# A graph layer on one core: row loads of SP taken out, 100 chunks of columns each on ScalarE and VectorE

## The chip, the cores and the metric

The kernel runs on one core of a Trainium2 chip. The time is the device time of one execution in microseconds (us); of several executions the median is given. The engines are named as the profile names them: PE (TensorE matmul, with its weight loads as PEld), DVE (VectorE), ACT (ScalarE), POOL (GpSimd) and SP (SyncE, which issues transfers). Each works through its own list of instructions in order.

## What is computed

One layer of a graph network over 12,500 nodes of 128 features and 200,000 edges that are sorted by their target `dst`:

```
h = maximum(layernorm(x), 0)
msgs = h[src]
agg = segment_sum(msgs, dst) / maximum(degree(dst), 1)
h = relu(agg @ Wg + h @ Ws + bg)          # 128 -> 128
h = tanh(h @ W1 + b1)                     # 128 -> 512
h = tanh(h @ W2 + b2)                     # 512 -> 512
out = x + h @ W3 + b3                     # 512 -> 128
```

All of it is in fp32. The inputs fix the edges, but the kernel may not rely on their values; it reads `src` and `dst` from memory.

## The kernel before

**Chunks.** The edges are cut into 1563 chunks of 128 (`NCH`). For each chunk the 128 rows `h[src]` have to be in SBUF, one edge to a partition. PE then multiplies them by a one-hot tile of 128 x 24 (`oh`, made by DVE for eight chunks at a time) and so adds them to the sums of the nodes of the current block. A block is 512 nodes, about 64 chunks, with smaller ones at the end (`blocks`). Sums of chunks that reach over two blocks are kept apart (`edge`).

**The start.** DVE and ACT normalise all rows in pieces and write them to a table in DRAM, `htab`. POOL meanwhile gathers the raw rows of ten groups of eight chunks (`raw_rows`, line 178), which are normalised later on DVE. After that the rows of `htab` are read back by blocks and turned on PE, and ACT copies them to `tab` (`own_turned`, line 700), a table in SBUF with the nodes along the free axis: one column of `tab` is one node's row.

**Four ways to the rows of a chunk.** They are what the change is about.

- *A gather* (line 385): POOL issues one indirect DMA a chunk, which fetches 128 rows of `htab` by the indices in `scol`. Tiles `rows`, `AHEAD` of them, and the gathers are written `AHEAD` chunks ahead of their use. 1323 chunks go this way.
- *Row loads* (`row_loads`, line 414): SP reads 32 offsets into registers and issues one transfer of 512 bytes for each row. 14 chunks. Tiles `srows`.
- *Column copies* (`column_copies`, line 435): ACT reads 16 offsets into registers and copies one column of `tab` for each edge, a 128 x 1 copy, into a tile `cols1`; `turn` (line 455) has PE transpose it and ACT copy the result to `turned`. 50 chunks.
- *Column pairs* (`column_pairs`, line 445): DVE reads 16 offsets and writes two columns with each of eight instructions into `cols2`; the second column of each pair is a sum of both, which `turn` undoes with a second matmul (`minus`). 96 chunks.

Every fourth chunk between `FROM` and `UNTIL` that isn't raw is a slot for one of the last three ways; `SHARES` says how many each gets, and they are spread evenly (lines 125 to 134).

**The order.** It is written out by hand in one loop over the chunks (line 882). `behind` counts the gathered chunks that PE has passed in this order. `load_times` (line 833) gives each group of copies a place in it: ACT's copies for a chunk stand between the chunk before of the same engine and the chunk itself, 18 gathers earlier (`MARGIN`), DVE's pairs 26 earlier (`MARGIN + GRP`). A block is turned nine gathers ahead of its use (line 849). The layers of a block begin `LEAD` chunks after its last chunk (line 926) and go on by one step in every two chunks (line 946). From chunk 1312 (`QUICK`) on, the steps are placed by a small sum of due times (line 918), since no more blocks follow to fill the time.

Of the kernel before, what the change touches and what calls it, by code (L numbers as in the profile page):

```python
# [22 lines left out]
F32 = mybir.dt.float32  # L23
# [8 lines left out]
P = 128  # L32
# [8 lines left out]
AHEAD = 24  # L41
LATE = 28
LEAD = 16
# [4 lines left out]
SHARES = 14, 50, 96  # L48
FROM, UNTIL = 104, 1540
SBUFS = 4  # L50
MARGIN = 18
TOGETHER = 4
LOADS = 32, 16, 16
# [24 lines left out]
def windowed(ctx, tc, x, src, dst, Wg, Ws, bg, W1, b1, W2, b2, W3, b3, out, flag):  # L78
# [46 lines left out]
    lanes = ([], [], [])  # L125
# [22 lines left out]
    rows_one = ctx.enter_context(tc.tile_pool(name="rows_one", bufs=SBUFS))  # L148
# [54 lines left out]
    ROWB = 4 * D  # L203
    places = [const.tile([NROW, CPR // EVERY, P], I32, name=f"place{i}") for i in range(2)]
# [37 lines left out]
    with tc.tile_pool(name="ln", bufs=2) as ln:  # L242

        def indices(name, a, pad, keep):
            r = sp.tile([NROW, ROW], I32, name="idx_raw")

            nc.vector.memset(r, pad)
            even = FULL // 16 * 16
            for s0, s1 in ((0, even), (even, FULL)):
                if s1 > s0:  # L250
                    nc.scalar.dma_start(r[s0:s1, :], a[s0 * ROW : s1 * ROW].rearrange("(p e) -> p e", e=ROW))
            nc.scalar.dma_start(r[FULL : FULL + 1, :REST], a[FULL * ROW : E].rearrange("(p e) -> p e", p=1))
            if name == "src":
                some = r.rearrange("r (q p) -> r q p", p=P)[:, AT::EVERY]
                nc.vector.tensor_scalar(places[0], some, float(ROWB), None, op0=ALU.mult)
                nc.vector.tensor_scalar(
                    places[1].rearrange("r q (i t) -> r q t i", t=2), some.rearrange("r q (t i) -> r q t i", t=2),
                    4.0, float(TAB_AT), op0=ALU.mult, op1=ALU.add,
                )
            else:  # L260
                r8 = sp.tile([NROW, ROW], U8, name="r8")
                nc.scalar.copy(r8, r.bitcast(U8).rearrange("r (e b) -> r e b", b=4)[:, :, 0])
                end = ahead_of + NROW * ROW
                nc.scalar.dma_start(bytes_at[ahead_of:end].rearrange("(r e) -> r e", e=ROW), r8)
                past = sp.tile([1, max(ahead_of, past_end)], U8, name="past")
                nc.vector.memset(past, PAST)
                nc.scalar.dma_start(bytes_at[:ahead_of].rearrange("(o e) -> o e", o=1), past[:, :ahead_of])
                nc.scalar.dma_start(bytes_at[end:].rearrange("(o e) -> o e", o=1), past[:, :past_end])
            rf = sp.tile([NROW, ROW], F32, name="idx_f")
            nc.vector.tensor_copy(rf, r)  # L270
            if name == "dst":
                by_chunk = rf.rearrange("r (q p) -> r q p", p=P)
                nc.vector.tensor_copy(firsts, by_chunk[:, :, 0])
                base = sp.tile([NROW, CPR], F32, name="base")
                nc.vector.tensor_tensor(base, firsts, lo, op=ALU.max)
                nc.vector.tensor_tensor(base, base, hi, op=ALU.min)
                nc.vector.tensor_copy(bases, base)
                nc.vector.tensor_tensor(  # L278
                    by_chunk, by_chunk, base[:, :, None].to_broadcast([NROW, CPR, P]), op=ALU.subtract
                )  # L280
            for q0 in range(0, CPR, 4):
                p = ps_m.tile([P, 4, P], F32, name="pm")
                for q in range(4):
                    nc.tensor.transpose(p[:, q, :NROW], rf[:, (q0 + q) * P : (q0 + q + 1) * P], ident[:NROW, :NROW])  # L284
                keep(q0, p[:, :, :NROW].rearrange("p q r -> p r q"))
# [73 lines left out]
    hbytes = htab.rearrange("n d -> (n d)").bitcast(U8)  # L359
# [34 lines left out]
    def offsets(lane, c, p0):  # L394
        step, first_at = (4, TAB_AT) if lane else (ROWB, 0)
        r, q = divmod(c, CPR)
        kind = (mybir.EngineType.SP, mybir.EngineType.Activation, mybir.EngineType.DVE)[lane]
        loads, vs = nc.values_load_multi_w_load_instructions(
            places[min(lane, 1)][r : r + 1, q // EVERY, p0 : p0 + LOADS[lane]], engines=[kind], min_val=first_at,
            max_val=first_at + (N - 1) * step,  # L400
            skip_runtime_bounds_check_because="src holds rows of x, as the indirect DMAs take it to",
        )
        for ld in loads:
            if lane == 2 and last:
# [5 lines left out]
        if lane:  # L410
            vs = [v.with_bounds(min_val=first_at, max_val=first_at + (N - 1) * step, guaranteed_mod_val=0, out_of_modulus=4) for v in vs]
# [15 lines left out]
    def two(lane, c, p0):  # L427
# [3 lines left out]
        for p in range(p0, p0 + LOADS[lane], 2):  # L431
            a, b = (tab[:, bass.ds((at_v[q] - TAB_AT) // 4, 1)] for q in (p, p + 1))
            yield p, by_pair[:, p // 2], a, b

    def column_copies():
        for c in lanes[1]:
            columns[c] = ed.tile([P, P], F32, name="cols1", bufs=3)
            for p0 in range(0, P, LOADS[1]):
                for p, to, *ab in two(1, c, p0):
# [5 lines left out]
    def column_pairs():  # L445
        for c in lanes[2]:
            columns[c] = ed.tile([P, P], F32, name="cols2", bufs=4)
            for p0 in range(0, P, LOADS[2]):
                for p, to, a, b in two(2, c, p0):
# [5 lines left out]
    def turn(c):  # L455

        pt, both = ps_m.tile([P, 4, P], F32, name="pm"), columns.pop(c)
        if c in lanes[1]:
# [374 lines left out]
    def load_times(lane):  # L833
# [12 lines left out]
    loading = [  # L846
        (loads, list(load_times(i))) for i, loads in enumerate((row_loads(0), column_copies(), column_pairs()))
    ]
    turns = sorted((max(1, sum(o < c for o in order) - MARGIN // 2), c) for c in sum(lanes[1:], []))
# [32 lines left out]
    for c in range(NCH):  # L882
# [14 lines left out]
        if c % (GRP // 2) == 0 and g + 2 < ngrp:  # L897
            copies, times = loading[2]
            while times and times[0] <= behind:
                times.pop(0)  # L900
                next(copies, 0)
# [6 lines left out]
        if not raw(c) and c not in apart:  # L908
            behind += 1
            for rows_of_lane, times in loading[:2]:  # L910
                while times and times[0] <= behind:
                    times.pop(0)
                    next(rows_of_lane, 0)
# [414 lines left out]
```

## Time and profile before

| | us |
|---|---|
| median of 3 runs | 1784.79 |
| lowest, highest run | 1784.59, 1784.84 |
| the profiled execution | 1782.46 |
| its span, first to last instruction | 1780.6 |
| POOL busy | 1334.6 |
| PE busy | 1424.5 |
| DVE busy | 1214.6 |
| ACT busy | 898.5 |

All figures of the engines below come from the one profiled execution. Busy times are the time in which at least one instruction of the engine ran. Matmuls overlap, and their ends are modelled, so that PE's busy time overstates how near it is to its peak. Register loads and the issue of transfers do not count as busy; a gap that they leave is put down to "issue". In a row of the timeline stand the start, the duration, the engine, the line, the operation, the tiles and the count, and in brackets the idle time ahead of it with what ended it. A row of the waits reads: who waited for what, us in total, times, the longest. A row of a stretch has the busy time of each engine with its instructions, and at its end the granted PE clock, the DMA share and GB/s; where one line was asked for, only its engine stands there.

### The profile page before, as it was taken

To read this page: it belongs to the slowest core of one execution; us is meant where nothing else is said; L and a number is where in the kernel's file an instruction comes from. 1 tells how busy PE (TensorE), PEld (TensorE's weight loads), DVE (VectorE), ACT (ScalarE), POOL (GpSimd) and SP (SyncE) were. 2 spreads that over 40 slices of the span, in tenths; PEclk is the share of its full clock that TensorE was granted. 3 is DMA by queue.
4 is the path that set the end of the run, shared out by engine and by line. 5 is a ranking of instruction groups with operands and counts; after the bars stand their busy time and mean duration, and the time that the engine had idled before them with its cause. 6 is when DMAs were issued, how large, how long until landed. Compare 5 with 4: busy or idle time off the path is not lost.

```text
span 1780.6 us, 35578 instructions
## 1 busy us (share of the span) xinstructions
PE 1424.5 (80%) x5696; PEld 942.3 (53%) x5696; DVE 1214.6 (68%) x6958; ACT 898.5 (50%) x6963; POOL 1334.6 (75%) x1411
## 2 busy tenths in 40 slices
PE   0047577878888898888988898888899899889798
PEld 0036455555555555455655655545556555555577
DVE  7965586786678676876768768777578675676520
ACT  1212254646546455554645545665546655656443
POOL 7777777777777777777777777777777777777774
PEclk9999999868877887986877877889778787889699
DMA  8945222222222222222222222222222222222221
GB/s 205 248 131 140 61 59 65 62 65 74 60 73 72 69 64 72 66 69 70 74 61 71 73 61 71 75 58 74 70 62 72 72 73 63 66 70 66 65 59 47
DMA packets 132964, 139.20 MB, mean 78 GB/s; under 512 B 31655, under 2 KB 109347, under 8 KB 132536
## 3 DMA queue, kind: packets, MB, share of 16 engines
q0 software_dynamic: 44896, 92.04, 20.5%
q1 hardware_dynamic: 84558, 41.29, 8.6%
q10 hardware_dynamic: 3276, 3.51, 0.7%
q14 instruction: 181, 1.48, 0.3%
q8 instruction: 53, 0.87, 0.2%
HBM read 123.71 MB, written 13.03 MB: 77 GB/s over the span
## 4 chain that ended last, share of the span: by engine, by line
PE 50%; DMA 28%; issue 14%; DVE 3%; POOL 3%; ACT 1%; SPq 0%; DVEq 0%; POOLq 0%; ACTq 0%
PE pm L377 35%; DMA rows<-htab,scol 25%; PE agg L377 11%; PE edge L377 4%; POOL rows L387 3%; DMA xt<-in_x_dram 2%; PE pm L380 1%; DVE cols L450 1%; DVE h L240 1%; DVE agg L226 1%; DVE agg L233 0%; DMA xb<-htab 0%; ACT h L472 0%; ACT cols L441 0%; DMA htab<-h 0%
## 5 line engine op out<-in xcount | busy, mean ns | idle before, releaser
L387 POOL DMA_INDIRECT rows<-htab,scol x1323 | 1253.8, 948 | 403.3 <-issue 225.6
L450 DVE SCALAR_TENSOR_TENSOR cols<-first_only,tab 128x2 f32<-128x2 f32 x6144 | 886.3, 218 | 222.9 <-issue 213.4
L377 PE MATMUL pm<-h,w 128*128 128x512 f32 (+4 forms) x1344 | 770.0, 673 | 2.8 <-ACT h L472 2.6
L441 ACT COPY cols<-tab 128x1 f32 x6400 | 652.2, 188 | 74.5 <-issue 67.0
L377 PEld LDWEIGHTS agg<-oh,rows 128*128 128x128 f32 x1914 | 382.7, 244 | 435.3 <-DMA rows<-htab,scol 256.8
L377 PE MATMUL agg<-oh,rows 128*128 128x24 f32 x1914 | 391.0, 303 | 176.8 <-DMA rows<-htab,scol 170.4
L377 PEld LDWEIGHTS pm<-h,w 128*128 128x128 f32 x1344 | 234.5, 220 | 15.2 <-issue 10.2
L377 PEld LDWEIGHTS edge<-oh,rows 128*128 128x128 f32 x732 | 138.0, 228 | 170.1 <-DMA rows<-htab,scol 100.2
L377 PE MATMUL edge<-oh,rows 128*128 128x24 f32 x732 | 146.3, 291 | 74.4 <-DMA rows<-htab,scol 69.8
L472 ACT ACTIVATE h<-pm,b2c 128x512 f32<-128x512 f32 (+4 forms) x112 | 70.8, 632 | 255.8 <-PE pm L377 254.8
L494 DVE TENSOR_TENSOR oh<-shared,dloc 128x192 f32<-128x192 f32 x186 | 65.0, 351 | 187.5 <-PE agg L377 109.1
L475 ACT COPY turned<-pm 128x128 f32<-128x128 f32 x146 | 38.1, 261 | 124.5 <-PE pm L377 101.7
L178 POOL DMA_INDIRECT raw<-in_x_dram,rsrc x80 | 80.0, 1000 | 25.8 <-issue 23.5
L472 ACT ACTIVATE h<-pm,b1c 128x512 f32<-128x512 f32 (+4 forms) x112 | 69.4, 631 | 43.9 <-PE pm L377 43.2
L534 DVE TENSOR_SCALAR_CACHE_REDUCE nearby<-nearby,parity 128x656 uint8<-128x656 uint8 x98 | 87.0, 887 | 0.0
L284 PE MATMUL pm<-ident,idx_f 98*128 98x98 f32 x32 | 5.7, 373 | 82.6 <-DVE idx_f L278 54.0
L472 ACT ACTIVATE h<-pm,b3c 128x512 f32<-128x512 f32 (+4 forms) x28 | 17.7, 633 | 94.1 <-PE pm L377 94.1
L377 PEld LDWEIGHTS agg<-oh,turned 128*128 128x128 f32 x194 | 43.7, 249 | 34.5 <-issue 33.0
L377 PE MATMUL pm<-ident,cols 128*128 128x128 f32 x192 | 51.6, 357 | 0.0
L377 PE MATMUL pm<-minus,cols 128*64 128x128 f32 x192 | 49.3, 345 | 0.0
L475 ACT COPY tab<-pm 128x512 f32<-128x512 f32 (+1 forms) x25 | 14.4, 577 | 68.8 <-PE pm L380 68.8
L284 PEld LDWEIGHTS pm<-ident,idx_f 98*128 98x128 f32 x32 | 5.2, 227 | 82.8 <-issue 54.2
(122 smaller groups left out, 904.9 us busy)
## 6 DMA issues: line engine op xcount, KB each, us to landing
srows<-htab SPq DMA_DIRECT2D x1792, 0.5 KB
rows<-htab,scol POOLq DMA_INDIRECT x1323
nearby<-bytes_at SPq DMA_DIRECT2D x98, 82.0 KB
xb<-htab SPq DMA_DIRECT2D x24, 256.0 KB
xb<-in_x_dram SPq DMA_DIRECT2D x23, 256.0 KB
out_dram<-o SPq DMA_DIRECT2D x23, 256.0 KB
xt<-in_x_dram SPq DMA_DIRECT2D x8, 640.0 KB
htab<-h SPq DMA_DIRECT2D x8, 640.0 KB
```

Source lines behind the costliest of these rows:

```text
L178: nc.gpsimd.indirect_dma_start(out=t[:, j, :], out_offset=None, in_=x, in_offset=bass.IndirectOffsetOnAxis(ap=rsrc[:, g, j : j + 1], axis=0),)
L226: nc.vector.tensor_reduce(stats[:, 0], xt, AX.X, ALU.add)
L240: nc.vector.scalar_tensor_tensor(h, xt, 0.0, spread(stats[:, 1], k), op0=ALU.max, op1=ALU.mult)
L377: tc.keep_in_program_order(nc.tensor.matmul(*a, **k))
L380: tc.keep_in_program_order(nc.tensor.transpose(*a, **k))
L387: nc.gpsimd.indirect_dma_start(out=r, out_offset=None, in_=htab, in_offset=bass.IndirectOffsetOnAxis(ap=scol[:, c : c + 1], axis=0),)
L441: tc.keep_in_program_order(nc.scalar.copy(to[:, t : t + 1], of))
L450: last[:] = [tc.keep_in_program_order(nc.vector.scalar_tensor_tensor(to, first_only, a, b.to_broadcast([P, 2]), op0=ALU.mult, op1=ALU.add))]
L472: tc.keep_in_program_order(nc.scalar.activation(*a, **k))
L475: tc.keep_in_program_order(nc.scalar.copy(*a))
L494: newest[:] = [nc.vector.tensor_tensor(oh[:, :k, :w], lane[:, None, :w].to_broadcast([P, k, w]), dloc[:, g * GRP : g * GRP + k][:, :, None ...
L534: done = nc.vector.tensor_scalar(w, w, parity[:, t % 2 : t % 2 + 1], None, op0=ALU.is_equal, op1=ALU.add, accum_out=found[:, t : t + 1])
```

## The change

Five settings change: `AHEAD` 24 to 30, `LEAD` 16 to 24, `FROM` 104 to 80, `SHARES` from 14, 50, 96 to 100, 100, and `LOADS` to 16 alone. SP's row loads and all that served them are taken out: the tiles `srows`, the second table of offsets with its DVE instruction, and their due times. The lanes are renumbered, ACT's columns from 1 to 0 and DVE's from 2 to 1. The code of the copies themselves stays. There are 345 slots now, the first in use chunk 87 on ACT and 91 on DVE; before, 339 and chunks 119 and 111. The last chunk of ACT is 1531 and of DVE 1535 in both.

```diff
-AHEAD = 24
+AHEAD = 30
 LATE = 28
-LEAD = 16
+LEAD = 24
...
-SHARES = 14, 50, 96
-FROM, UNTIL = 104, 1540
-SBUFS = 4
+SHARES = 100, 100
+FROM, UNTIL = 80, 1540
 MARGIN = 18
 TOGETHER = 4
-LOADS = 32, 16, 16
+LOADS = 16
...
-        kind = max(range(4), key=lambda k: owed[k])
+        kind = max(range(3), key=lambda k: owed[k])
         owed[kind] -= len(slots)
-        if kind < 3:
+        if kind < 2:
             lanes[kind].append(c)
...
-    rows_one = ctx.enter_context(tc.tile_pool(name="rows_one", bufs=SBUFS))
...
-                nc.vector.tensor_scalar(places[0], some, float(ROWB), None, op0=ALU.mult)
...
-    def row_loads(lane):
-        for c in lanes[lane]:
-            r = rows_one.tile([P, D], F32, name="srows")
-            rows_t[c] = r
-            rb = r.bitcast(U8)
-            for p0 in range(0, P, LOADS[0]):
-                for p, v in offsets(lane, c, p0):
-                    sp_dma(rb[p : p + 1, :], hbytes[bass.ds(v, ROWB)].rearrange("(o b) -> o b", o=1))
-                    if (p + 1) % TOGETHER == 0:
-                        yield
...
     def column_copies():
-        for c in lanes[1]:
+        for c in lanes[0]:
             columns[c] = ed.tile([P, P], F32, name="cols1", bufs=3)
...
     def column_pairs():
-        for c in lanes[2]:
+        for c in lanes[1]:
             columns[c] = ed.tile([P, P], F32, name="cols2", bufs=4)
...
-        use = [max(FROM - 46 + MARGIN, use[0] - step), *use] if lane else [use[0] - step * k for k in range(SBUFS - 1, 0, -1)] + use
-        if lane == 0:
-            use = [max(u, FROM // 2 + 7 * step // 8 * i) for i, u in enumerate(use)]
-        some = LOADS[2] if lane == 2 else TOGETHER
+        use = [max(FROM - 46 + MARGIN, use[0] - step), *use]
+        some = LOADS if lane else TOGETHER
         for i in range(len(lanes[lane])):
             for k in range(P // some):
-                yield max(1, use[i] + (use[i + 1] - use[i]) * k * some // P - (0, MARGIN, MARGIN + GRP)[lane])
+                yield max(1, use[i] + (use[i + 1] - use[i]) * k * some // P - (MARGIN + GRP if lane else MARGIN))
```

What it does to the lists of the engines, at three places. A row is a line of the program, an operation, the tile written and the one read, the size, and a count where it repeats; the line numbers of the changed kernel are smaller, by 18 near the copies.

POOL, from the last raw groups through all gathers of rows. Before:

```order
L178 DMA raw_156<-in_x_dram,rsrc 128x128 x8
L178 DMA raw_165<-in_x_dram,rsrc 128x128 x8
L178 DMA raw_174<-in_x_dram,rsrc 128x128 x8
L178 DMA raw_183<-in_x_dram,rsrc 128x128 x8
L387 DMA rows<-htab,scol 128x128 x1323
```

Now:

```order
L176 DMA raw_153<-in_x_dram,rsrc 128x128 x8
L176 DMA raw_162<-in_x_dram,rsrc 128x128 x8
L176 DMA raw_171<-in_x_dram,rsrc 128x128 x8
L176 DMA raw_180<-in_x_dram,rsrc 128x128 x8
L382 DMA rows<-htab,scol 128x128 x1283
```

The raw groups are as they were; 40 gathers are gone.

ACT, where the table is complete and the columns begin (`place` are the offsets that go to registers). Before:

```order
L475 COPY tab<-pm 128x512 x24
L475 COPY tab<-pm 128x256
L475 COPY sums<-edge 128x280
L475 COPY rd<-pm 128x512
L398 TENSOR_LOAD place_203
L441 COPY cols_1578<-tab 128x1 x16
```

Now:

```order
L457 COPY tab<-pm 128x512 x24
L457 COPY tab<-pm 128x256
L393 TENSOR_LOAD place
L423 COPY cols_1287<-tab 128x1 x16
L393 TENSOR_LOAD place
L423 COPY cols_1287<-tab 128x1 x16
```

The first copies stood behind the sums of the first block and its degrees, and now stand right behind the table.

ACT again, in the layers of the ninth block, from its first activation to the next one. Before:

```order
L472 ACTIVATE h_512_26993<-pm,bgc 128x512
L441 COPY cols_25892<-tab 128x1 x12
L398 TENSOR_LOAD place_203
L441 COPY cols_25892<-tab 128x1 x16
L398 TENSOR_LOAD place_203
L441 COPY cols_27264<-tab 128x1 x8
L472 ACTIVATE h_512_26997<-pm,b2c 128x512
```

Now:

```order
L454 ACTIVATE h_512_33401<-pm,bgc 128x512
L393 TENSOR_LOAD place
L423 COPY cols_33349<-tab 128x1 x16
L393 TENSOR_LOAD place
L423 COPY cols_33349<-tab 128x1 x8
L457 COPY turned<-pm 128x128
L423 COPY cols_33349<-tab 128x1 x8
L393 TENSOR_LOAD place
L423 COPY cols_33349<-tab 128x1 x16
```

Before, 36 copies and two register loads stand between the two activations. Now 88 copies, six loads and a turned block do, of which the piece shows the first 48 copies; the next activation, `h_512_33405<-pm,b2c`, comes after 40 more.

More of the change, by code (lines that the diff above doesn't have):

```diff
@@ L202, in windowed @@
     scol = const.tile([P, NCOL], I32, name="scol")
-    ROWB = 4 * D
-    places = [const.tile([NROW, CPR // EVERY, P], I32, name=f"place{i}") for i in range(2)]
+    place_of = const.tile([NROW, CPR // EVERY, P], I32, name="place")
     dloc = const.tile([P, NCOL], F32, name="dloc")
@@ L403, in offsets @@
         for ld in loads:
-            if lane == 2 and last:
+            if lane and last:
                 tc.add_manual_dep(
@@ L409, in offsets @@
             tc.keep_in_program_order(ld)
[L410 to L411 removed]
+        vs = [v.with_bounds(min_val=TAB_AT, max_val=most, guaranteed_mod_val=0, out_of_modulus=4) for v in vs]
         return enumerate(vs, p0)
[L414 to L423 removed]
     columns, last = {}, []
@@ L430, in two @@
         at_v = dict(offsets(lane, c, p0))
-        for p in range(p0, p0 + LOADS[lane], 2):
+        for p in range(p0, p0 + LOADS, 2):
             a, b = (tab[:, bass.ds((at_v[q] - TAB_AT) // 4, 1)] for q in (p, p + 1))
@@ L435, in column_copies @@
     def column_copies():
-        for c in lanes[1]:
+        for c in lanes[0]:
             columns[c] = ed.tile([P, P], F32, name="cols1", bufs=3)
-            for p0 in range(0, P, LOADS[1]):
-                for p, to, *ab in two(1, c, p0):
+            for p0 in range(0, P, LOADS):
+                for p, to, *ab in two(0, c, p0):
                     for t, of in enumerate(ab):
@@ L897, in windowed @@
         if c % (GRP // 2) == 0 and g + 2 < ngrp:
-            copies, times = loading[2]
+            pairs, times = loading[1]
             while times and times[0] <= behind:
                 times.pop(0)
-                next(copies, 0)
+                next(pairs, 0)
         while c % GRP == GRP // 2 and counted < len(blocks) and reach[counted][-1] // GRP <= g + (c >= QUICK):
@@ L909, in windowed @@
             behind += 1
[L910 to L913, printed above, removed]
+            copies, times = loading[0]
+            while times and times[0] <= behind:
+                times.pop(0)
+                next(copies, 0)
             while turns and turns[0][0] <= behind:
```

24 lines of the change are left out of this document (10 added, 14 removed).

## The prediction

> **What bounds the kernel now.** I read the head of the page first, then the costliest groups, then the busy time by stage.
>
> ```profile
> span 1780.6 us, 35578 instructions
> PE 1424.5 (80%) x5696; PEld 942.3 (53%) x5696; DVE 1214.6 (68%) x6958; ACT 898.5 (50%) x6963; POOL 1334.6 (75%) x1411
> L387 POOL DMA_INDIRECT rows<-htab,scol x1323 | 1253.8, 948 | 403.3 <-issue 225.6
> L450 DVE SCALAR_TENSOR_TENSOR cols<-first_only,tab 128x2 f32<-128x2 f32 x6144 | 886.3, 218 | 222.9 <-issue 213.4
> L441 ACT COPY cols<-tab 128x1 f32 x6400 | 652.2, 188 | 74.5 <-issue 67.0
> ```
>
> By shares PE looks like the bound. The timeline of POOL says otherwise:
>
> ```profile
> 1000.27 0.94 POOL L387 DMA_INDIRECT rows<-htab,scol  x1 [0.30 <-PE pm L377]
> 1009.01 0.94 POOL L387 DMA_INDIRECT rows<-htab,scol  x1 [0.30 <-PE pm L377]
> ...
> 1763.46 0.94 POOL L387 DMA_INDIRECT rows<-htab,scol  x1 [0.30 <-PE pm L377]
> ```
>
> The rows are the first and the last of eight gathers in a row near 1000 us, and the last of all. Each has 0.94 us of work and 0.30 us ahead of it, whatever is named as the releaser. From the first row to the second are seven steps: (1009.01 - 1000.27) / 7 = 1.2486 us a gather. POOL never pauses longer; its 75% is a full engine whose 0.30 us is the price of an issue. PE has room, as its waits show:
>
> ```profile
> PE agg L377 <- DMA rows<-htab,scol: 170.4, 236, 8.4
> PE edge L377 <- DMA rows<-htab,scol: 69.8, 99, 2.2
> PE pm L377 <- ACT h L472: 3.9, 8, 1.5
> ACT h L472 <- PE pm L377: 445.0, 196, 12.8
> ```
>
> PE waits 240.2 us for gathered rows and 3.9 us for ScalarE; ScalarE waits 445.0 us for PE in its activations alone. So the number of gathers times their step sets the end.
>
> **The change part by part.** *Fewer gathers.* 160 chunks had their rows by another way (14 on SP, 50 on ACT, 96 on DVE), now 200 have. The gathers go from 1323 to 1283: 40 x 1.2486 = 49.9 us off POOL. The span would be 1780.6 - 49.9 = 1730.7 us if nothing else holds POOL up. That is a floor, since the step itself is not touched.
>
> *ScalarE's columns, 50 chunks to 100.* This is the edit that can take the gain back. ACT now has 12,800 single-column copies and 800 register loads (one ahead of 16 copies) where it had 6,400 and 400. Their price, from stretches in which ACT did not wait for PE:
>
> ```profile
> 432.11 0.25 ACT L475 COPY turned<-pm 128x128 f32<-128x128 f32 x1
> 432.27 0.68 ACT L472 ACTIVATE h<-pm,b1c 128x512 f32<-128x512 f32 x1
> 432.85 4.79 ACT L441 COPY cols<-tab 128x1 f32 x48
> 437.55 0.26 ACT L475 COPY turned<-pm 128x128 f32<-128x128 f32 x1
> ...
> 173.80 0.37 ACT L475 COPY tab<-pm 128x256 f32<-128x256 f32 x1 [0.67 <-PE pm L380]
> ...
> 211.00:1710.00 1499.00, 1289.45 (x4967) 827.62 (x4968) 1070.74 (x6716) 840.04 (x6844) 1133.16 (x1201) 0.82 0.26 67
> 211.00:1710.00 1499.00, 652.15 (x6400) 0.82 0.26 67
> ```
>
> 48 copies, with their loads between them, take from 432.85 to 437.55: 97.9 ns each. The last two rows are the stretch that holds every copy, first for all engines, then for the copies alone: ACT's other work there is 840.0 - 652.2 = 187.8 us. There are 52 more copies of turned blocks in the changed stretch at 0.16 us (432.11 to 432.27): 8 us, so 196.
>
> Gaps that the register loads leave visible come on top:
>
> ```profile
> 422.77 1.21 ACT L441 COPY cols<-tab 128x1 f32 x12 [0.54 <-issue]
> 440.26 1.21 ACT L441 COPY cols<-tab 128x1 f32 x12 [0.17 <-issue]
> ```
>
> These two are all the gaps in the longest stretch without a wait for PE (421.65 to 441.47, 156 copies): 0.71 us, which for 12,800 copies makes 58 us. The ends: below, no gaps, 12,800 x 97.9 ns + 196 = 1449 us; above, the mean of the whole run doubled, busy 2 x 652.2 and gaps 2 x 67.0, + 196 = 1634 us. I take 1253 + 196 + 58 = 1507 us, near the lower end, because many of the 67.0 us stand behind a wait for PE, and an engine that is late does not wait.
>
> What ACT has for it: the copies may begin when the table is whole, at 174.2 us (173.80 + 0.37). The last chunk of ACT, 1531, has its copies due 48 gathers before POOL's last, which moves to 1763.5 - 49.9 = 1713.6 us, so at 1713.6 - 48 x 1.2486 = 1653.7 us. PE turns the block nine gathers after that, 11.2 us of grace. Together 1491 us. So ACT is 16 us over by my value, 42 us under by the low end, 143 us over by the high one. **ACT and POOL come out level**, and I charge 16 us. Behind a late copy on ACT stand the activations of the layers, and behind these PE's next matmuls; what is late next is the freeing of row buffers, and so POOL.
>
> The Trainium skill ("DMA: Bandwidth & Descriptors", section "Latency and other measured facts") speaks against this sum: it gives a register load a floor of about 600 ns. As an estimate from that page 800 loads would be 480 us, ACT 1253 + 196 + 480 = 1929 us, and the run about 2170 us. The x48 row has three loads between its copies and no room for it, so the trace here doesn't show that cost on a busy ACT.
>
> *VectorE's columns, 96 to 100.* DVE works in groups of 8 pairs behind one register load:
>
> ```profile
> 1408.18 1.21 DVE L450 SCALAR_TENSOR_TENSOR cols<-first_only,tab 128x2 f32<-128x2 f32 x8 [0.30 <-issue]
> 1409.65 1.14 DVE L450 SCALAR_TENSOR_TENSOR cols<-first_only,tab 128x2 f32<-128x2 f32 x8 [0.25 <-issue]
> 211.00:1700.00 1489.00, 882.82 (x6120) 0.82 0.26 68
> ```
>
> 1.47 us a group, 800 groups, 1176 us. Its other work is at most 1070.7 - 882.8 = 188 us between 211 and 1710 (the first number from the row of all engines above), and at most the 37 us from 174 to 211: 1401 us. It may take from 174.2 us until the turning of its last chunk, 1535, that is 36 gathers before POOL's last: 1713.6 - 36 x 1.2486 = 1668.6, so 1494 us. Cost nothing, with 93 us to spare; without that cover four chunks would cost 4 x 8 x 1.47 = 47 us.
>
> *Turning on PE.* 54 more chunks are turned: 50 of ACT by one transpose, four of DVE by two matmuls.
>
> ```profile
> L380 PE MATMUL pm<-ident,cols 128*128 128x128 f32 x50 | 17.1, 341 | 0.0
> L377 PE MATMUL pm<-ident,cols 128*128 128x128 f32 x192 | 51.6, 357 | 0.0
> L377 PE MATMUL pm<-minus,cols 128*64 128x128 f32 x192 | 49.3, 345 | 0.0
> ```
>
> 17.1 + 4/96 x (51.6 + 49.3) = 21.3 us. It lies in the 240.2 us of waiting for rows; if that were used up, 21.3 us is its price.
>
> *SP's row loads.* 1792 small transfers go. POOL does not wait for their landing or for SP, so they are worth nothing on POOL's path. *30 gathers ahead* gives POOL 6 x 1.2486 = 7.5 us more lead; POOL has no wait to shorten, so 0, but it softens a late ACT. *Layers 24 chunks late*: eight chunks are four more steps of layer work left for the end.
>
> ```profile
> 859.02 1.10 PE L377 MATMUL pm<-h,w 128*128 128x512 f32 x2
> 860.32 1.10 PE L377 MATMUL pm<-h,w 128*128 128x512 f32 x2
> 1700.00:1781.00 81.00, 71.48 (x476) 59.68 (x474) 5.87 (x34) 28.42 (x105) 48.87 (x52) 0.97 0.21 53
> ```
>
> A step at full clock is 1.30 us, so 5.2 us; the last 81 us leave PE 9.5 us. I take 0; the price without that room is 5.
>
> **The sum.** 1780.6 - 49.9 + 16 = 1746.7 us of span. The profiled execution took 1782.46 us, 1.9 above its span, and the median of the runs is 1784.79, 2.3 above that: 1746.7 + 4.2 = 1751 us.
>
> **The rivals.** *A, ACT becomes the bound.* The mechanism: the latency of the loads stands open, as after a block that waits for PE.
>
> ```profile
> ACT cols L441 <- issue: 67.0, 134, 0.9
> ```
>
> For it: 134 of the 400 loads left a gap, 0.5 us each. Against: the run of 48. With the mean busy copy and the gaps of the long stretch ACT needs 1304 + 196 + 58 = 1558 us, 67 over, 1802 us; with the upper end 143 over, 1878 us; I name 1840. It turns the sign where ACT needs more than 1491 + 50 = 1541 us, so above (1541 - 196) / 12,800 = 105.1 ns a copy with all gaps; I count on 102.4. Its far end is a gap of 0.5 us at each of the 800 loads: 1253 + 196 + 400 = 1849 us, 358 over, 2093 us; it has 0.01 of the chance. The Trainium skill's floor for a load, above, would be this far end and 80 us more.
>
> *B, PE's slow phases are no longer made good.*
>
> ```profile
> 807.13 2.06 PE L377 MATMUL pm<-h,w 128*128 128x512 f32 x2
> 809.69 2.06 PE L377 MATMUL pm<-h,w 128*128 128x512 f32 x2
> 804.00:812.00 8.00, 7.88 (x19) 4.78 (x20) 1.78 (x10) 0.71 (x6) 5.94 (x7) 0.50 0.23 60
> 860.00:866.00 6.00, 6.00 (x31) 3.99 (x30) 4.56 (x28) 5.95 (x58) 4.47 (x6) 1.00 0.25 66
> 300.00:1700.00 1400.00, 1220.45 (x4742) 777.65 (x4742) 1000.16 (x6311) 787.64 (x6400) 1058.23 (x1122) 0.81 0.26 68
> ```
>
> At a granted clock of 0.50 a step of two chunks takes 2.56 us, at 1.00 it takes 1.30 us, and 0.81 in the mean makes 38% of the time slow. In the changed stretch (chunks 83 to 1539: 1457 chunks, 1177 gathers) POOL needs 1177 / 1457 x 2 x 1.2486 = 2.02 us for two chunks. 728 steps x 0.38 x 0.54 us = 149 us fall behind and are made good at full clock, now only as fast as ACT goes, 1507 / 728 = 2.07 us. Should half stay, the run takes 1730.7 + 75 + 4.2 = 1810 us. For it: ACT and PE wait for each other in order. Against: the 3.9 us that PE waited for ACT, and up to 30 rows in hand.
>
> The Trainium skill ("TensorE: Matmul & The Clock Gate", "The HAM clock gate") says that the array falls to half its clock after some 3.4 us of idling and comes back after as long a busy time. The two clocks are in the rows above. By that rule a PE held up by ACT in pieces would be slow longer, which is this rival.
>
> *C, the gain is handed back at the end*: PE has more layer work left and POOL's 49.9 us are spent there: 1785 us, as before. Against: the tail above has room for four steps.
>
> *That the change doesn't do what it says* is out: the order shows 1283 gathers.
>
> **How the numbers follow.** Forecast 0.66, within 1735 (no overhang) to 1780; A 0.18; B 0.12; C 0.04. About 0.2% is what a measurement can tell, 3.6 us. Faster is the forecast, 0.66. Same is C and a sliver of B, 0.05. Slower is the rest, 0.29. The range starts at the floor, 1730.7 + 4.2 = 1735, and to hold 8 in 10 takes in C, most of B and the near part of A: up to 1820. The time is the forecast's, 1751.
>
> **What would show it.** POOL right: 1283 gathers, still 0.30 us ahead of each, the last near 1715 to 1735. ACT right: busy about 1500 us, its waits for PE's matmuls down from 445.0 to under 100 us, copies at 98 to 102 ns. A: gaps on "issue" ahead of the copies above 130 us, and POOL pausing on PE. B: a granted clock under 0.81 between 300 and 1650 us and PE waiting for ACT by tens of us. C: the last gather near 1715 with over 40 us behind it. Wrong outright: a gather step other than 1.25 us, or DVE's pairs holding PE up.

## The result and the profile after

| | us |
|---|---|
| median of 4 runs | 1753.88 |
| lowest, highest run | 1752.09, 1758.59 |
| the kernel before, same job | 1784.69 |
| ratio | 0.9835, interval 0.9814 to 0.9857 |
| the profiled execution, its span | 1753.46, 1751.4 |

The change makes the kernel 1.65% faster; 1751 us was forecast. The span is 4.7 us above the forecast one (1746.7) and 20.7 us above the floor (1730.7).

The page of the changed kernel: busy times, the three groups that answer to those shown of before, and the chain by engine.

```profile
PE 1384.8 (79%) x5740; PEld 926.2 (53%) x5762; DVE 1253.5 (72%) x7213; ACT 1495.0 (85%) x13417; POOL 1296.7 (74%) x1371
ACT 31%; DMA 27%; PE 24%; issue 6%; DVE 5%; POOL 4%; ACTq 2%; DVEq 0%; SPq 0%; POOLq 0%
L382 POOL DMA_INDIRECT rows<-htab,scol x1283 | 1216.4, 948 | 391.0 <-DMA rows<-htab,scol 164.0
L423 ACT COPY cols<-tab 128x1 f32 x12800 | 1274.0, 188 | 31.8 <-issue 22.0
L432 DVE SCALAR_TENSOR_TENSOR cols<-first_only,tab 128x2 f32<-128x2 f32 x6400 | 923.1, 217 | 257.8 <-issue 243.2
```

The chain by engine of the kernel before:

```profile
PE 50%; DMA 28%; issue 14%; DVE 3%; POOL 3%; ACT 1%; SPq 0%; DVEq 0%; POOLq 0%; ACTq 0%
```

ACT goes from the emptiest of PE, DVE, ACT and POOL to the fullest, and into the chain that ended last: 31%, where it had 1%. The copies take 1274.0 / 12,800 = 99.5 ns each. The idle time ahead of POOL's gathers is 391.0 / 1283 = 0.30 us each, so POOL still never pauses. The last of POOL's gathers and the last of ACT's columns, from the timelines:

```profile
1713.04 0.94 POOL L382 DMA_INDIRECT rows<-htab,scol  x1 [0.30 <-issue]
1679.82 4.80 ACT L423 COPY cols<-tab 128x1 f32 x48
```

The last gather starts at 1713.0 us (1713.6 was worked out). So POOL's 50 us came in full, and the 20.7 us above the floor lie behind it: from the end of the last gather to the end of the run are 37.4 us now, 16.2 before. What PE does there, and what it waited for ahead of it, shows where they come from. First the busy times behind the last gather, in the kernel before and in the changed one (PE's is the first number after the length):

```profile
1764.40:1780.60 16.20, 9.46 (x74) 8.29 (x72) 0.43 (x3) 4.33 (x14) 0.01 (x1) 0.87 0.06 16
```

```profile
1714.00:1752.00 38.00, 31.55 (x274) 30.60 (x272) 1.30 (x8) 14.94 (x47) 0.00 (x0) 0.99 0.05 15
```

PE has 31.6 us of work left when the last rows are on their way, and had 9.5. Most of it is matmuls of the layers (26.0 us, where it was 6.9), first before, then after:

```profile
L377 PE MATMUL pm<-h,w 128*128 128x100 f32 (+1 forms) x56 | 6.9, 278 | 0.4 <-ACT h L472 0.4
L372 PE MATMUL pm<-h,w 128*128 128x128 f32 (+2 forms) x192 | 26.0, 283 | 1.0 <-ACT h L454 1.0
```

Now its waits between 1400 and 1700 us, before and after:

```profile
PE agg L377 <- DMA rows<-htab,scol: 16.1, 21, 2.6
PE edge L377 <- DMA rows<-htab,scol: 13.1, 19, 2.2
...
PE pm L377 <- ACT h L472: 2.6, 4, 1.5
```

```profile
PE pm L372 <- ACT h L454: 33.5, 14, 5.8
...
PE agg L372 <- DMA rows<-htab,scol: 3.5, 4, 1.1
```

Before, PE was ahead and waited 29.2 us for rows there. Now it waits 33.5 us for ScalarE's activations and hardly ever for rows: it falls behind POOL. The 30 tiles of rows are deep enough that POOL does not notice, so what PE did not get done stands at the end.

How far PE falls behind can be read off the trace, since two matmuls use the rows of each gather. The last two of the run, before and after:

```profile
1766.40 0.40 PE L377 MATMUL agg<-oh,rows 128*128 128x24 f32 x2
1738.50 0.31 PE L372 MATMUL agg<-oh,rows 128*128 128x24 f32 x2
```

They start 2.0 us behind the end of the last gather before, and 24.5 us behind it now. From there to the end of the run it takes no longer than it did: 12.9 us, and 14.2 before. So the 20.7 us are this lag of PE. The same difference for every gather says where it arises. Over chunks 1280 to 1311 PE is 2.9 us behind in the mean (2.6 before), so up to there it makes good what it loses; over chunks 1400 to 1539 it is 24.6 us behind (4.7 before).

### The profile page after: what moved, and what is told of

Its sections match the earlier page's. It is cut to its first block, busy times and chain, and to the rows that moved or that the text cites. A ratio compares the mean times of both kernels' runs of the same rounds, so it can differ in the third digit from the quotient of the medians.

```text
span 1751.4 us, 39095 instructions
## 1 busy us (share of the span) xinstructions
PE 1384.8 (79%) x5740; PEld 926.2 (53%) x5762; DVE 1253.5 (72%) x7213; ACT 1495.0 (85%) x13417; POOL 1296.7 (74%) x1371
## 4 chain that ended last, share of the span: by engine, by line
ACT 31%; DMA 27%; PE 24%; issue 6%; DVE 5%; POOL 4%; ACTq 2%; DVEq 0%; SPq 0%; POOLq 0%
ACT cols L423 26%; DMA rows<-htab,scol 25%; PE pm L372 17%; PE agg L372 5%; POOL rows L382 4%; ACT h L454 3%; ACTq L393 2%; PE edge L372 2%; DMA xt<-in_x_dram 1%; DVE cols L432 1%; DVE h L237 1%; ACT turned L457 1%; DVE agg L223 1%; DVE agg L230 1%; PE pm L375 1%
## 5 line engine op out<-in xcount | busy, mean ns | idle before, releaser
L382 POOL DMA_INDIRECT rows<-htab,scol x1283 | 1216.4, 948 | 391.0 <-DMA rows<-htab,scol 164.0
L423 ACT COPY cols<-tab 128x1 f32 x12800 | 1274.0, 188 | 31.8 <-issue 22.0
L432 DVE SCALAR_TENSOR_TENSOR cols<-first_only,tab 128x2 f32<-128x2 f32 x6400 | 923.1, 217 | 257.8 <-issue 243.2
L372 PE MATMUL pm<-h,w 128*128 128x512 f32 (+4 forms) x1344 | 743.3, 652 | 29.4 <-ACT h L454 26.6
L372 PEld LDWEIGHTS agg<-oh,rows 128*128 128x128 f32 x1858 | 365.5, 243 | 377.7 <-DMA rows<-htab,scol 194.9
L372 PE MATMUL agg<-oh,rows 128*128 128x24 f32 x1858 | 368.3, 300 | 143.8 <-DMA rows<-htab,scol 136.7
L372 PE MATMUL edge<-oh,rows 128*128 128x24 f32 x708 | 133.3, 282 | 59.1 <-DMA rows<-htab,scol 56.1
L176 POOL DMA_INDIRECT raw<-in_x_dram,rsrc x80 | 79.5, 994 | 25.6 <-issue 24.1
L372 PEld LDWEIGHTS agg<-oh,turned 128*128 128x128 f32 x266 | 58.5, 245 | 42.3 <-issue 38.7
L372 PE MATMUL agg<-oh,turned 128*128 128x24 f32 x266 | 55.0, 289 | 1.1 <-ACT turned L457 1.1
L372 PE MATMUL pm<-ident,h 128*128 128x128 f32 (+1 forms) x196 | 41.3, 295 | 13.7 <-ACT h L454 13.6
```

What stands on the lines that cost most here:

```text
L176: nc.gpsimd.indirect_dma_start(out=t[:, j, :], out_offset=None, in_=x, in_offset=bass.IndirectOffsetOnAxis(ap=rsrc[:, g, j : j + 1], axis=0),)
L372: tc.keep_in_program_order(nc.tensor.matmul(*a, **k))
L382: nc.gpsimd.indirect_dma_start(out=r, out_offset=None, in_=htab, in_offset=bass.IndirectOffsetOnAxis(ap=scol[:, c : c + 1], axis=0),)
L423: tc.keep_in_program_order(nc.scalar.copy(to[:, t : t + 1], of))
L432: last[:] = [tc.keep_in_program_order(nc.vector.scalar_tensor_tensor(to, first_only, a, b.to_broadcast([P, 2]), op0=ALU.mult, op1=ALU.add))]
```

## The experiments

Three theories of the 20.7 us were put to the test: **A**, ScalarE has more work than time over the whole run; **Q**, it keeps up until chunk 1312 (`QUICK`), where the steps of the layers begin to follow close on each other, and loses behind it; **L**, the later start of the layers (`LEAD`) leaves work for the end. The runs fell on several chips. In the first profile's and two other jobs the kernel before takes 1782 to 1785 us, on two other chips 2165 and 2188 us, so only ratios to the kernel before in the same job are compared.

### Where the kernel before takes 2165 to 2188 us

The changed kernel itself, with no edit:

> The changed kernel once more, since in the four runs above the kernel before took 2165 us and not 1785, with ACT's and DVE's instructions coming in pieces with 0.5 to 1.2 us between them that no wait explains. If that belongs to the place where they ran and not to the kernels, the kernel before is at 2165 us here again or back at 1785; at 1785 the changed kernel is at 1754, at 2165 it is near the three variants of it above, 2400 to 2450 us, since it has 12,800 copies on ACT that come singly.

Measured: 2480.26 us against 2187.88, ratio 1.1343 (1.1292 to 1.1393), a little above the 2400 to 2450 us that were expected. There the same change makes the kernel 13% slower. Two groups of its page, then its waits, then a stretch of ACT and a gather of POOL:

```profile
L382 POOL DMA_INDIRECT rows<-htab,scol x1283 | 1218.4, 950 | 1113.2 <-PE agg L372 533.1
L423 ACT COPY cols<-tab 128x1 f32 x12800 | 1369.7, 188 | 615.9 <-issue 601.8
```

```profile
ACT cols L423 <- issue: 601.8, 1092, 1.2
PE pm L372 <- ACT h L454: 251.5, 67, 13.3
PE agg L372 <- ACT turned L457: 172.4, 29, 22.1
```

```profile
1020.19 0.19 ACT L423 COPY cols<-tab 128x1 f32 x1 [0.44 <-issue]
1020.91 0.28 ACT L423 COPY cols<-tab 128x1 f32 x2 [0.52 <-issue]
1022.32 2.01 ACT L423 COPY cols<-tab 128x1 f32 x18 [1.13 <-issue]
```

```profile
1012.35 0.95 POOL L382 DMA_INDIRECT rows<-htab,scol  x1 [8.86 <-PE agg L372]
```

These are all the signs that the prediction named for rival A: gaps on "issue" ahead of the copies (601.8 us, against 22.0 where the change is a gain), PE waiting for ACT, and POOL pausing on PE (8.86 us in the last row). ACT's copies need 1369.7 + 615.9 = 1986 us instead of 1306. The gather itself is as elsewhere, 0.95 us. But the mechanism is not the one that A named. What opens the gaps is not the register loads alone: there are 1092 gaps for 800 loads, single copies stand apart within a group of 16, and a load takes 1.04 us in the median, as it does where the change is a gain.

The kernel before, on such a chip, with SP's 14 chunks gathered instead:

```diff
-SHARES = 14, 50, 96
+SHARES = 0, 50, 96
```

> The kernel before, with SP's 14 chunks gathered by POOL and nothing else changed: the part of the change that takes the row loads out, alone. If the number of gathers times their step sets the end: 14 x 1.2486 = 17.5 us more, 1802 us. If SP's 1792 small transfers cost POOL or the gathers something, less than that, down to 1785 us.

Measured: ratio 0.9995 (0.9976 to 1.0015). It says less than was meant: 14 more gathers cost nothing because POOL waits there anyway (747.4 us ahead of 1337 gathers, 0.56 us each). Its waits show that the gaps belong to where it ran and not to the change, since its columns are those of the kernel before:

```profile
ACT cols L441 <- issue: 545.0, 893, 1.8
DVE cols L450 <- issue: 438.6, 877, 1.9
```

Before, on the chip of the first profile, these were 67.0 and 213.4 us. Two settings put back alone, and four chunks moved from ScalarE to VectorE:

```diff
-LEAD = 24
+LEAD = 16
```

> The changed kernel with the layers 16 chunks late instead of 24. The profile after shows POOL's last gather at 1713.0 us and the end 38 us behind it (17 us before the change). Theory A (ACT is over its time: 1507 us of work against 1491) and theory Q (ACT keeps up until the layers run close behind each other, from chunk 1312 on, and loses there by round trips with PE): both say 1750 to 1758 us, the end still 35 to 40 us behind the last gather. Theory L (the eight chunks of delay leave layer work for the end): 1740 us or less, the end 17 to 28 us behind the last gather.

```diff
-AHEAD = 30
+AHEAD = 24
```

> The changed kernel with 24 row tiles instead of 30. If ACT is the last to finish by some 20 us and PE therefore uses rows late, POOL runs out of free tiles earlier and its last gather comes later than 1713 us, but the end, which ACT sets, stays: 1752 to 1758 us. If the 30 tiles are what makes the change possible, POOL stands still in the middle too, with waits far over 0.30 us, and the time is 1762 us or more.

```diff
-SHARES = 100, 100
+SHARES = 96, 104
```

> The same 200 chunks, four of them moved from ACT to DVE: ACT has 4 x 14.3 us (128 copies at the 99.5 ns that the profile after shows, a turn, gaps) less, about 52 us, DVE 47 us more. Theory A: ACT is then 36 us under its time, the overhang is gone, the end 17 us behind the last gather, 1732 to 1740 us. Theory Q: only the part of it in the last 300 us helps (10 us of ACT's work), 1742 to 1748 us. If DVE has less room than the 93 us I found: 1755 us or more, with DVE's columns holding PE up.

Measured: 1.1285 (1.1262 to 1.1308), 1.1319 (1.1279 to 1.1359) and 1.1096 (1.1047 to 1.1144). The first two lie within or beside the interval of the unedited change. Only the third moves the time: by 0.019 to 0.022 against the first two, which shared its chip, so 10 to 12 us for each chunk taken off ScalarE (0.019 x 2165 / 4 = 10.3). The expectations assumed a chip on which POOL sets the end. What follows: there ScalarE sets the pace, or stands next to what does.

### Where the kernel before takes 1783 us

**Register loads of 32** in place of 16, for ScalarE alone:

```diff
-LOADS = 16
+LOADS = 32, 16
...
-            for p0 in range(0, P, LOADS):
+            for p0 in range(0, P, LOADS[0]):
```

> The changed kernel with ScalarE's register loads of 32 offsets: 400 loads in place of 800, the copies as they were. Where the kernel before takes about 1785 us: the loads left 22.0 us of gaps ahead of the copies, so A expects up to 11 us off ScalarE and a ratio of 0.977 to 0.984; Q and L expect 0.982 to 0.986. Where the kernel before takes about 2165 us: if it is the latency of the loads that opens the gaps of some 560 to 600 us ahead of ScalarE's copies, they fall to about 300 us and the ratio from 1.13 to 1.03 or less; if the instructions themselves arrive late, the gaps stay above 500 us and the ratio at 1.11 to 1.14.

Measured: 2031.6 us against 1782.74, ratio 1.1396 (1.1381 to 1.141). All three theories missed: half as many loads were expected to change next to nothing, and cost 280 us. The waits and a row of the timeline:

```profile
ACT cols L423 <- issue: 323.8, 368, 2.0
POOL rows L382 <- PE agg L372: 308.1, 326, 9.6
```

```profile
800.75 3.06 ACT L423 COPY cols<-tab 128x1 f32 x32 [0.95 <-issue]
```

Nearly each of the 400 loads now stands open, for 323.8 / 368 = 0.88 us. The loads themselves say why. Here they are with 32 offsets, with 16 (the change) and with 8 (the next run), with the shortest, the median and the longest in ns:

```profile
L393 ACTq TENSOR_LOAD <-place x400: 1938/2014/2581, 172.0 to 1956.4; - x134
L393 ACTq TENSOR_LOAD <-place x800: 1004/1044/1740, 173.2 to 1681.9; - x160
L393 ACTq TENSOR_LOAD <-place x1600: 535/557/1143, 172.5 to 1677.5; - x178
```

A load takes the longer the more offsets it has. It is under way while ScalarE still works on the copies ahead of it: in the traces it starts 1.09 us before these end (the median, with 16 offsets and with 32 alike). That covers the 1.04 us of a load of 16 and leaves 0.9 us of one of 32 open. Why it does not start earlier, no run tells. The Trainium skill ("DMA: Bandwidth & Descriptors", section "Latency and other measured facts") has a floor of about 600 ns for a register load. The loads of 8 come out just below it, at 0.56 us, and those of 16 and 32 well above it, so here the number of offsets counts; and the runs with 8 and 16 show that the time need not be paid on a busy engine.

**Loads of 8**, by the same edit with another number:

```diff
-LOADS = 16
+LOADS = 8, 16
```

> The changed kernel with ScalarE's register loads of 8 offsets: 1600 loads in place of 800. Loads of 32 opened a gap of 0.88 us at 368 of 400 loads, loads of 16 one of 0.3 us at 75 of 800. If a load is hidden as long as its registers and those still being read fit side by side, loads of 8 are hidden too, and what they cost is at most their own issue: 800 more at under 0.03 us each (the run of 48 copies had no room for more), so where the kernel before takes about 1785 us a ratio of 0.982 to 0.995. If instead a load has a latency that 8 copies at 0.098 us (0.78 us) do not cover, 1600 gaps of 0.1 us open, 160 us in all, and the ratio is 1.05 to 1.08. Where the kernel before takes about 2165 us: 1.13 to 1.17 if the gaps there are those of the loads, 1.12 to 1.14 if it is the instructions that arrive late.

Measured: ratio 0.9831 (0.9814 to 0.9848), the first branch, since a load of 8 is covered as well. The waits:

```profile
ACT cols L423 <- issue: 9.3, 35, 0.5
```

ACT's columns with the gaps ahead of them take 1258.6 + 12.3 = 1271 us by the page, 35 less than with loads of 16 (1274.0 + 31.8 = 1306), and the runs are as fast as the change's. Work taken off ACT isn't returned one for one.

**Four chunks from ScalarE to VectorE** (the edit to 96 and 104 above):

> The changed kernel with four chunks moved from ScalarE to VectorE (96 and 104). Where the kernel before takes about 1785 us: A expects ScalarE's need to fall by 4 x 128 x 0.118 = 60 us of its own time at the far price and 50 us at that of a row of copies, so all of its 30 us of lateness goes: ratio 0.970 to 0.975, with VectorE at 1448 of 1494 us. Q expects half of it, 0.975 to 0.981. L expects 0.983 to 0.986. Where the kernel before takes about 2165 us: A expects 1.105 to 1.115.

Measured: 1746.61 us against 1782.74, ratio 0.9798 (0.9785 to 0.981). That is the fastest of all kernels, and its interval lies just below the change's. A's 0.970 to 0.975 missed, Q's half was hit, L missed. 50 us less work bought some 7 us: PE ends 18.3 us behind the last gather instead of 24.5.

**`LEAD` back to 16:**

> The changed kernel with the layers beginning 16 chunks late, as before, in place of 24. Where the kernel before takes about 1785 us: L expects the 20.7 us at the end to shrink by at least 5.2 us (four steps at 1.30 us), a ratio of 0.975 to 0.981. A and Q expect nothing or a small loss, since a later layer lets ScalarE's activations come when PE is ready: 0.982 to 0.990. Where the kernel before takes about 2165 us: A expects 1.125 to 1.135.

Measured: ratio 0.983 (0.9818 to 0.9843), not to be told from 0.9835, and outside L's range. L falls.

**`QUICK` later:**

```diff
-QUICK = 1312
+QUICK = 1440
```

> The changed kernel with QUICK at 1440 in place of 1312: the steps of the last layers keep the even pace of one step in two chunks for 128 chunks longer. Where the kernel before takes about 1785 us, the changed one stands at a ratio of 0.9835. Theory Q (ScalarE keeps up until the layers run close behind each other from chunk 1312 on, and loses its 30 us there): ScalarE's copies end some 15 us earlier, PE's waits for ScalarE between 1400 and 1700 us fall from 38 us to under 25, ratio 0.970 to 0.980. Theory A (ScalarE has more work than time everywhere): the copies end where they did, ratio 0.983 to 0.990. Theory L (layer work is left for the end): more is left, ratio 0.986 to 0.995. Where the kernel before takes about 2165 us (ScalarE's copies come with gaps there): A says no change against the changed kernel, ratio 1.12 to 1.14.

Measured: ratio 0.9891 (0.9876 to 0.9905), outside Q's range and inside A's and L's. Its timeline and its busy times behind the last gather:

```profile
1667.95 1.20 ACT L423 COPY cols<-tab 128x1 f32 x12
```

```profile
1711.70:1757.80 46.10, 40.09 (x300) 37.28 (x298) 1.11 (x8) 17.89 (x54) 0.00 (x0) 0.96 0.04 12
```

The copies end 15 us earlier, as Q said and A did not (1669 against 1684.6 us). Q's other sign is there too: PE's waits for ScalarE's activations between 1400 and 1700 us fall from 33.5 to 13.4 us. PE's lag moves with the setting: over chunks 1360 to 1439 it is 3.0 us in the mean, where it was 19.2 in the change, and it rises behind chunk 1440, to 11.2 us at the last gather. But the layer steps that were put off are not made good: PE has 40.1 us of work behind the last gather, 8.5 more.

**The same 100 and 100, tilted**: three of ScalarE's chunks moved from behind chunk 1312 to ahead of it.

```diff
-SHARES = 100, 100
+EARLIER, LATER = (87, 80), (13, 20)
...
+    for some, share in (([c for c in slots if c < QUICK], EARLIER), ([c for c in slots if c >= QUICK], LATER)):
```

> The changed kernel with the same 100 and 100 chunks, but three of ScalarE's 16 chunks behind chunk 1312 given to VectorE, and three of VectorE's ahead of it given to ScalarE: 87 and 80 ahead of 1312, 13 and 20 behind it. Where the kernel before takes about 1785 us (the changed one at 0.9835, 96 and 104 chunks at 0.9798): theory A (ScalarE has more work in all than time) expects no change, 0.982 to 0.986. Theory Q (it keeps up until chunk 1312 and loses behind it) expects up to 3 x 128 x 0.098 = 38 us less work in the last 250 us, so that most of the 20.7 us at the end goes: 0.972 to 0.979. If ScalarE is as full ahead of chunk 1312 as behind it, the 38 us turn up there, POOL begins to pause, and the ratio is above 0.99. Where the kernel before takes about 2165 us: 1.12 to 1.14 by both.

Measured: ratio 0.9914 (0.9901 to 0.9927). Q's 0.972 to 0.979 is missed; the third branch is hit in its number, though POOL did not pause. PE's largest waits for ScalarE from 174 to 1300 us, here and in the changed kernel:

```profile
PE pm L373 <- ACT h L455: 41.6, 24, 4.2
PE agg L373 <- ACT turned L458: 20.6, 12, 4.0
PE pm L373 <- ACT turned L458: 19.6, 11, 4.7
```

```profile
PE pm L372 <- ACT h L454: 17.6, 11, 3.1
```

ACT has 38 us more to do there, and PE is already behind: its waits for ACT rise to 81.8 us in these rows, from 19.6 (17.6 and 2.0 for `turned`), and over chunks 1280 to 1311 it is 24.1 us behind its gathers, where it was 2.9. So ACT has no room ahead of chunk 1312 to take more work: this is what Q had wrong.

**96 and 104, tilted:**

```diff
-EARLIER, LATER = (87, 80), (13, 20)
+EARLIER, LATER = (85, 83), (11, 21)
```

> 96 and 104 chunks, tilted in the same way: 85 and 83 ahead of chunk 1312, 11 and 21 behind it, where 96 and 104 evenly spread had 16 and 17 behind it. Where the kernel before takes about 1785 us: Q expects below 0.9798, 0.970 to 0.977, with ScalarE's last copies ahead of 1665 us and the end 20 to 25 us behind the last gather. A expects 0.978 to 0.982, as with the even spread. If VectorE's 21 chunks behind 1312 are too many for the time there (21 x 8 x 1.47 = 247 us of some 245), PE waits for its blocks and the ratio is 0.98 to 0.99. Where the kernel before takes about 2165 us: 1.10 to 1.12.

Measured: ratio 0.9806 (0.9792 to 0.9819), as with the even spread: inside A's range and the third branch's. Q missed. Its waits of PE from 1400 to 1700 us:

```profile
PE pm L373 <- DVE mT L671: 24.5, 3, 14.6
...
PE pm L373 <- ACT h L455: 4.8, 7, 2.1
```

The wait for ScalarE is nearly gone, 4.8 us, and one for VectorE stands in its place, 24.5 us. In the longest of these waits, 14.6 us up to 1649 us, VectorE works through pairs without a pause but those for their loads, and `mT`, the mean of a block, comes behind them in its list: 21 chunks of pairs in that stretch are too many for it.

**All together.** From each kernel's trace, in us; "behind" is the time from the end of a gather to the first matmul on its rows, as a mean over chunks 1280 to 1311 and for the last gather:

| kernel | last gather ends | behind, 1280 to 1311 | behind, last gather | from there to the end | PE busy behind the last gather | span |
|---|---|---|---|---|---|---|
| before | 1764.4 | 2.6 | 2.0 | 14.2 | 9.5 | 1780.6 |
| the change | 1714.0 | 2.9 | 24.5 | 12.9 | 31.6 | 1751.4 |
| 96 and 104, tilted | 1715.7 | 10.7 | 15.3 | 13.0 | 22.5 | 1744.0 |
| 96 and 104 | 1713.2 | 2.4 | 18.3 | 13.2 | 25.6 | 1744.6 |
| loads of 8 | 1714.3 | 3.0 | 19.3 | 13.2 | 26.7 | 1746.9 |
| `LEAD` 16 | 1714.5 | 4.3 | 20.2 | 13.4 | 27.4 | 1748.0 |
| tilted | 1713.4 | 24.1 | 29.3 | 13.2 | 36.2 | 1756.0 |
| `QUICK` 1440 | 1711.7 | 3.4 | 11.2 | 35.0 | 40.1 | 1757.8 |

In all but the last row the kernels differ only in how late PE is at the last gather; from there to the end it is always 13 to 14 us. So the loss is PE's lag, and for the changed kernel its place is settled too: all of it arises behind chunk 1312, where the layer steps follow close on each other and PE waits 33.5 us for ScalarE's activations, and it moves with `QUICK`. That is Q's place. A fails as an account of it, since PE is on time until there and with `QUICK` 1440 for longer, though ScalarE has the same work; L fails with `LEAD` 16. What Q had wrong is the remedy: ScalarE has no room ahead of chunk 1312 (tilted), and steps that are put off are missing at the end (35.0 us from the last rows on). What relieves ScalarE lowers the lag, but 35 to 50 us off it take only 5 to 6 us off (19.3 and 18.3 us), and with ScalarE out of the way behind 1312, VectorE takes its place. Why 96 and 104 chunks still leave 13 to 16 us more than before (15.3 and 18.3 against 2.0) is only in part known: PE's waits for activations between 1400 and 1700 us are still 26.6 us with the even spread. The turning of 54 more chunks on PE is part of the kernel in all of these rows but the first, and no run took it away.

## Why the prediction was right, by its steps

- *Fewer gathers*, 40 x 1.2486 us: right. 1283 gathers with 0.30 us ahead of each, the last 0.6 us from where it was put.
- *ScalarE 16 us over, and charged in full*: near in size, 20.7 us, but by luck. The copies were over at 1684.6 us, 19.7 behind the 1664.9 (1653.7 + 11.2) that the sum allowed, and the parts were off and cancelled: copies and gaps took 1306 us (1311 predicted), ACT's other work 1431.7 - 1269.4 = 162 us (196 predicted), and in the place of these stood waits for PE, which the sum left out (45.8 us in the activations over the run). Nor is the excess charged one for one: with four chunks fewer ScalarE was some 50 us lighter, which by this sum takes all of it away, and the time fell by 7 us. The sum sets all of ScalarE's work against all of its time; the cost came from one stretch, behind chunk 1312, where the layer steps follow close on each other, and the sum has no term for that.
- *Behind a late copy, the activations, then PE, then the row buffers and POOL*: right as far as PE; POOL was never reached, since the rows in hand outlasted the delay. Its last gather came at 1713.0 us, ahead of the 1715 to 1735 that the prediction named, and the cost showed up as PE's lag behind it.
- *VectorE at nothing*: right; 923.1 + 257.8 = 1181 us, 1176 predicted. The 93 us to spare held for four more chunks, while 21 behind chunk 1312 were too many.
- *Turning on PE in the waits for rows*: these fell from 240.2 to 192.8 us over the run by the waits below, so they were not used up; but from 1400 us on 3.5 us were left of them, and the cover was gone there. Its price was not measured alone.
- *SP's loads, 30 gathers ahead, `LEAD`*: `LEAD` moved nothing where POOL sets the end. `AHEAD` and SP's chunks alone were run only where POOL waits on PE, so for the chip of the first profile they stay untested.
- *Rival A*: its mechanism is real. With loads of 32 it gives, by the prediction's own sum, 1253 + 196 + 324 = 1773 us for ACT, 282 over 1491, so 1730.7 + 282 + 4.2 = 2017 us; 2031.6 was measured. On two of the chips its signs decide too, by gaps that are not those of the loads: the copies with their gaps alone need 1986 us there, above the 1849 us that the prediction's far end gave to all of ScalarE's work. The prediction gave A 0.18 from one profile, which could not tell this.
- *Rival B*: out, though one of its signs is there (PE waits for ScalarE by tens of us). The granted clock from 300 to 1650 us rose from 0.81 to 0.83 (the row below), and from 1400 to 1700 us, where the lag arises, from 0.83 to 0.87; ahead of chunk 1312 PE still makes good what it loses. *Rival C*: PE's work at the end did grow, by 22 us instead of the four steps' 5.2, so the loss lies where C put it, with 37.4 us behind the last gather (over 40 was its sign), but not by `LEAD` and not to the whole of the gain: it is work that PE was late with, and the way from its last rows to the end did not grow.

The changed kernel's waits over the run; its busy times from 300 to 1650 us; and those from 174 to 1680 us, first for all engines, then for the copies alone:

```profile
PE agg L372 <- DMA rows<-htab,scol: 136.7, 178, 8.2
PE edge L372 <- DMA rows<-htab,scol: 56.1, 80, 1.8
PE pm L372 <- ACT h L454: 52.8, 30, 5.8
ACT h L454 <- PE pm L372: 45.8, 50, 3.7
...
ACT cols L423 <- issue: 22.0, 75, 0.7
```

```profile
300.00:1650.00 1350.00, 1162.67 (x4705) 750.17 (x4724) 1014.08 (x6385) 1294.78 (x11966) 1020.53 (x1082) 0.83 0.24 68
...
174.00:1680.00 1506.00, 1264.85 (x5057) 824.82 (x5079) 1127.05 (x7008) 1431.70 (x13251) 1139.04 (x1205) 0.83 0.24 67
...
174.00:1680.00 1506.00, 1269.44 (x12755) 0.83 0.24 67
```

ACT is busy 1294.8 of 1350 us, 96%. It hardly waits for PE any more (45.8 us, where it was 445.0), and PE begins to wait for it: 52.8 us, where it was 3.9.

## What to carry to other kernels

When one engine's steady step sets the end, taking steps off it moves its last step by exactly their time. It pays as much until the engine that takes over the work is as full: then look at how far the engine between them lags behind the steps, and from which stretch on, not at who pauses. A sum of work against time over the whole run misses a stretch in which the work comes close together. An engine filled to 96% with short copies behind register loads has its latencies hidden by a narrow margin (1.04 of 1.09 us here). A load twice as long opened them, on other chips gaps of another origin came, and either of them turned a gain of 1.65% into a loss of 13 to 14%. Leave such an engine the few chunks of room that another one still has (96 and 104 were better than 100 and 100 on both kinds of chip).

## What the runs showed of the hardware

- A register load on ScalarE took 0.56 us for 8 offsets, 1.04 for 16 and 2.01 for 32 (medians). It started some 1.09 us before the copies ahead of it ended, with 16 and with 32: so one of 32 stood open for 0.88 us, one of 16 hardly ever (22.0 us in all for 800), one of 8 even less (9.3 us for 1600).
- The same program differed from place to place by far more than from run to run: the kernel before took 1782 to 1785 us in three jobs, 2165 and 2188 us in two jobs on two other chips. Each of these chips was met in one job, so the runs do not tell whether it is the chip or the time. On the latter ScalarE's and VectorE's instructions came in pieces (545.0 and 438.6 us of gaps on "issue" ahead of the columns, where 67.0 and 213.4 were before), while a gather took the same 0.95 us. A load of 16 took 1.04 us in the median in both places. The granted clock was lower there too, 0.76 to 0.80 in the runs of the kernel before against 0.82 to 0.86; whether that is a cause or a consequence of PE's waiting is not shown. The traces do not show what supplied the instructions late; that stays open.
